# A two-block image kernel: softplus summed in PSUM, one product in ten moved from GpSimd to VectorE, large transfers cut into parts, background work spread

## The chip, the cores and the metric

The kernel runs on one core of a Trainium2 chip. The core has five engines with queues of their own: TensorE (PE, matrix products; the loading of its weights is listed apart as PEld), VectorE (DVE), ScalarE (ACT), GpSimd (POOL) and SyncE (SP, which here only issues transfers). Each engine works through its own list in order and waits on semaphores for the others. The metric is the device time of one execution in microseconds (us). It was 22,344.77 us in the median of three runs of the kernel before (22,316.2 to 22,348.97).

## The reference

The input is 16 images of 64 x 64 points with 96 channels, in float32. Two residual blocks follow one another. Each begins with a group normalisation of the image.

- Block one enlarges the image to twice its height and width by a band-limited interpolation, multiplies by a 384 x 96 matrix, applies a polynomial of degree two, multiplies by a 96 x 384 matrix, and filters and samples the result back to 64 x 64.
- Block two is a selective scan (a state-space layer). After a projection, a 3 x 3 convolution per channel and a SiLU, each image gives 192 channels of 4,096 points. They are read in four directions (rows, columns, and both backwards). In each direction there are 16 states per channel, and the recurrence along the 4,096 points is

```
delta = softplus(dts + bias)
h[t]  = exp(delta[t] * A) * h[t-1] + (delta[t] * u[t]) * B[t]
y[t]  = sum over the 16 states of h[t] * C[t]
```

The four results are added, normalised over the channels, multiplied by a gate, projected back to 96 channels and added to the image.

Only `softplus` and the product `h * C` are touched as arithmetic by the change. The kernel before and after computes softplus as max(s, 0) + ln(1 + e) - ((1 + e) - 1 - e) with e = exp(-|s|); the last term is the rounding error of 1 + e.

## The kernel before, in words

The time goes into `scan()` (lines 599 to 895). Everything else is either run before it (`front(0)`, the first image's preparation), after it (`finish(B - 1)`, the last image's end), or in the background of it.

**Units.** The work of the scan is cut into 3,072 units (`units`, line 699): 16 images, 8 steps in each (two pairs of directions times four pieces of 1,024 points), 6 blocks of channels and direction in a step, and 4 groups of states `j` in a block. A unit is a pair: two halves `e` of 128 partitions by 1,024 points. The loop at line 819 writes for each unit `n`, in this order:

- DVE: the recurrence of half 1 (`recur(n, 1, h)`, a TENSOR_TENSOR_SCAN at line 734 forwards or 736 backwards). Its decay `da` lies in PSUM, its drive `b` in SBUF, and it writes over `b`.
- PE: `read_out(n - 1)`, eight products that add the states of the unit before into `y` (line 758), then a background slot.
- ACT: `keep` (line 742), a copy of the last column of the state for the next piece, and `decay(n + 1, 1)` (line 719, exp of delta times A into one of two PSUM buffers).
- POOL: the product of half 1 with C (line 863, in place), and then `drive(n + 2)` (line 725, both halves of the drive of the unit after next, into one of three buffers `b`). This is "the odd product", and all that POOL does.
- DVE: the recurrence of half 0 (into the PSUM buffer of its decay), a second background slot, and the product of half 0 with C (line 873).
- ACT: `keep` and `decay(n + 1, 0)`; then a third slot.

A slot is thus met three times in a unit, at fixed places in the order of all engines.

**Background.** A slot advances generators by one `yield` (`Background`, lines 786 to 803). In each slot `project` of the next step may advance by one slice (60 slices spread over 58 slots, from the start of the step), and either `front` of the next image or, when that is done, `finish` of the image before may advance by one slice (404 slices over the 576 slots of an image). `front` and `finish` advance to the end when their result is due (`drain`).

**project** (lines 615 to 671) makes, for two halves of 512 points and three groups of channels, `delta` and `delta * u`. After a product on PE into `s` (line 643), each of these 768 projections runs through slots in order: ACT abs and exp (652, 653); ACT ln (655); DVE max and add (657); ACT 1 + e (659); DVE two operations (661, 662) that leave the softplus in PSUM; DVE times `u` (666); ACT copy (668); then both results are stored to memory through SP. The buffer `s` is single.

**front** and **finish.** `front` normalises (`norm`), runs block one in fine slices, then the convolution of block two (line 466, nine products for a tile, three in a slice). `finish` adds the four directions and does the output. Large transfers of up to 2 MB are single instructions on ACT's queue (`nc.scalar.dma_start`): the image `xt` (241), `s` (408), `x1` (431), `xs` (492), `ycol` (507, 508). All others are on SP's queue: the loads of `u` (627), the loads of `dtu` and `delta` (678) and of the rows B and C (687), and the stores of projections and results.

**Operands.** In the unit loop and in `project`, every DVE operation before has at most one input in SBUF; the other is in PSUM. Two small operations of the background have both in SBUF: `nb` (line 227, 96 x 1, twice an image) and `lin` (line 252, 96 x 96, once an image).

Of the kernel before, what the change touches and what calls it, by code (L numbers as in the profile page):

```python
# [70 lines left out]
POS = 3 * 8 * 6 * NQ  # L71
SLICES = 404
PSLICES = 60


@with_exitstack
def tile_two_blocks(
    ctx: ExitStack, tc: tile.TileContext,
    x, w1, w1t, b1, w2t, b2, coef, inpt, convw, convb, xpt, dtw, alog, dsk, onw, onb, opt,
    up, down, fold, ident, gmask, pmat, bumps, out,  # L80
# [29 lines left out]
    one_s = const.tile([128, 1], F32, name="one_s")  # L110
    nc.gpsimd.memset(one_s, 1.0)
    eps_g = const.tile([128, 1], F32, name="eps_g")
    nc.gpsimd.memset(eps_g, GEPS)
# [76 lines left out]
    def piece(shape, name):  # L190
        return b2p.tile(shape, F32, name=name, tag="piece")

    def norm(xt):

        s = small.tile([C, 8], F32, name="gs")
        for t in range(8):
            junk = piece([C, TB], "junk")
            nc.scalar.activation(junk, xt[:, TB * t:TB * t + TB], AF.Identity, accum_out=s[:, t:t + 1])
            if t % 2:
                yield  # L200
        yield
        m_ps = bank([C, 8], "m_ps")
        nc.tensor.matmul(m_ps, lhsT=gmask_s, rhs=s, start=True, stop=True)
        yield
        junk8 = small.tile([C, 8], F32, name="junk8")
        nmean = small.tile([C, 1], F32, name="nmean")
        nc.scalar.activation(junk8, m_ps, AF.Identity, scale=-1.0, accum_out=nmean)
        s2 = small.tile([C, 8], F32, name="gs2")
        for t in range(8):
            junk = piece([C, TB], "junk")  # L210
            nc.scalar.activation(
                junk, xt[:, TB * t:TB * t + TB], AF.Square, bias=nmean, accum_out=s2[:, t:t + 1]
            )
            if t % 2:
                yield
        yield
        v_ps = bank([C, 8], "v_ps")
        nc.tensor.matmul(v_ps, lhsT=gmask_s, rhs=s2, start=True, stop=True)
        yield
        var = small.tile([C, 1], F32, name="var")  # L220
        nc.scalar.activation(junk8, v_ps, AF.Identity, accum_out=var)
        rg = small.tile([C, 1], F32, name="rg")
        nc.scalar.activation(var, var, AF.Ln, bias=eps_g[0:C])
        nc.scalar.activation(rg, var, AF.Exp, scale=-0.5)
        nb = small.tile([C, 1], F32, name="nb")
        yield
        nc.vector.tensor_mul(nb, nmean, rg)
        yield
        return rg, nb

    def front(mi):

        x_c = x[mi].rearrange("h c w -> c h w")
        x_h = x[mi]
# [5 lines left out]
        xt = b16.tile([C, L], F32, name="xt", tag="b16")  # L240
        nc.scalar.dma_start(out=xt.rearrange("c (h w) -> c h w", w=HW), in_=x_c)
        for _ in range(4):
            yield
        rg, nb = yield from norm(xt)
# [160 lines left out]
        for _ in range(2):  # L405
            yield
        for i, on in enumerate((slice(0, JS), slice(JS, HW))):
            nc.scalar.dma_start(out=s[i], in_=s_d[:, on, :])
        for _ in range(8):
            yield  # L410
        x1 = xt
        x1v = x1.rearrange("c (h w) -> c h w", w=HW)
        done = None
        for j0 in range(0, HW + 8, 8):
# [15 lines left out]
            yield  # L430
        nc.scalar.dma_start(out=made["x1"], in_=x1)
        rg, nb = yield from norm(x1)
# [12 lines left out]
        for i, n, tiles, both in ((0, 128, 8, 0), (1, 64, 4, 4)):  # L445
            col = b16.tile([128, tiles * TB], F32, name="col", tag="b16")
            parts = [(n * k, t0) for k, t0 in enumerate((0, both)[:128 // n])]
            turned = None

            def turn(t, row, z):  # L450
                nc.scalar.copy(
                    col.rearrange("c (w h) -> c w h", w=HW)[:, :, 8 * t:8 * t + 8],
                    row.rearrange("c (h w) -> c w h", w=HW),
                )
                for p, t0 in parts:
                    cols = slice(TB * (t + t0), TB * (t + t0) + TB)
                    nc.sync.dma_start(out=made["xs"][2 * i, 0:n, cols], in_=row[p:p + n])
                    nc.sync.dma_start(out=made["z"][128 * i:128 * i + n, cols], in_=z[p:p + n])

            for t in range(tiles):  # L460
                c_ps = bank([128, 8, HW], "c_ps")
                for tap in range(9):
                    dy, dx = divmod(tap, 3)
                    for p, t0 in parts:
                        h0 = 8 * (t + t0) + dy
# [7 lines left out]
                    if tap % 3 == 2 and tap < 8:  # L473
                        yield
                z_ps = bank([128, 8, HW], "z_ps")
                for p, t0 in parts:
                    h0 = 8 * (t + t0) + 1
# [3 lines left out]
                    )  # L481
                yield
                row, z = piece([128, TB], "row"), piece([128, TB], "z")
# [3 lines left out]
                turned = t, row, z  # L487
                yield
            turn(*turned)
            yield  # L490
            if i == 0:
                nc.scalar.dma_start(out=made["xs"][1], in_=col)
            else:
                for p, t0 in parts:
                    to = made["xs"][2, 64:128, :].rearrange("c (w h) -> c w h", h=HW)
                    for w0 in range(0, HW, 16):
# [3 lines left out]
                        )  # L500
                        yield

    def finish(mi):

        y_d, xs_d, z_d, x1_d = (image[mi][k] for k in ("y", "xs", "z", "x1"))
        ycol = [b18.tile([128, L], F32, name="ycol0", tag="b18"), b16.tile([64, L], F32, name="ycol1", tag="b16")]
        nc.scalar.dma_start(out=ycol[0], in_=y_d[1, 0:128, :])
        nc.scalar.dma_start(out=ycol[1], in_=y_d[1, 128:DI, :])

# [9 lines left out]
        ahead = fetch_y(0)  # L519
        for _ in range(6):  # L520
            yield
        tail = None
        for t in range(8):
# [7 lines left out]
            for ob, n in ((0, 128), (1, 64)):  # L531
# [8 lines left out]
                if ob == 1:  # L540
                    sq.append(piece([128, TB], "sq"))
                    nc.scalar.activation(sq[0], yc[0], AF.Square)
                yield
                for i in range(2):
# [10 lines left out]
                yc.append(y_ps.rearrange("c h w -> c (h w)"))  # L555
                yield

# [3 lines left out]
            nc.tensor.matmul(v_ps, lhsT=mean_s, rhs=sq[0], start=True, stop=False)  # L561
            yield
            yz.append(piece([64, TB], "yz"))
            nc.vector.tensor_mul(yz[1], yc[1], z1)
            nc.tensor.matmul(v_ps, lhsT=mean_s[0:64], rhs=sq[1], start=False, stop=True)
            if t < 7:
                ahead = fetch_y(t + 1)
            yield
            r = sq[0][0:C]
# [3 lines left out]
            for i, n in ((0, 128), (1, 64)):  # L573
                nc.tensor.matmul(o_ps, lhsT=ow_s[0:n, i, :], rhs=yz[i], start=(i == 0), stop=(i == 1))
            yield
            e_ps = bank([C, TB], "oe_ps")
            for i, (w, of) in enumerate(((ob_s[:, 0, :], z0), (ob_s[0:64, 1, :], z1), (ident_s[0:C, 0:C], xt))):
                nc.tensor.matmul(e_ps, lhsT=w, rhs=of, start=(i == 0), stop=False)  # L578
            nc.vector.tensor_mul(r, o_ps, r)
            yield  # L580

# [9 lines left out]
        for _ in tail:  # L591
            yield

# [5 lines left out]
    def scan():  # L599


        with ExitStack() as es:
# [12 lines left out]
            def project(mi, pair, lc, out):  # L615
# [7 lines left out]
                for t in range(0, T, TB):  # L623
# [15 lines left out]
                    for i, v in enumerate((0, 2, 1)):  # L639
# [9 lines left out]
                        yield  # L649
                        e = pj.tile([128, TB], F32, name="e")  # L650
                        d = pj.tile([128, TB], F32, name="d")
                        nc.scalar.activation(e, s, AF.Abs)
                        nc.scalar.activation(e, e, AF.Exp, scale=-1.0)
                        yield
                        nc.scalar.activation(d, e, AF.Ln, bias=one_s)  # L655
                        yield
                        nc.vector.scalar_tensor_tensor(d, s, 0.0, d, ALU.max, ALU.add)  # L657
                        yield
                        nc.scalar.activation(s, e, AF.Identity, bias=one_s)
                        yield  # L660
                        nc.vector.scalar_tensor_tensor(s, s, -1.0, e, ALU.add, ALU.subtract)
                        nc.vector.tensor_sub(s, d, s)
                        yield
# [122 lines left out]
            class Background:  # L786


                def __init__(self, gen, slices, positions):
                    self.gen, self.slices, self.positions, self.at, self.n = gen, slices, positions, 0, 0  # L790

                def slot(self):
                    self.at += 1
                    if self.gen is not None and self.n * self.positions < self.at * self.slices:
                        self.n += 1
                        if next(self.gen, 0) == 0:
                            self.gen = None

                def drain(self):
                    while self.gen is not None:  # L800
                        self.n += 1
                        if next(self.gen, 0) == 0:
                            self.gen = None

# [14 lines left out]
            for n, (st, bi, j) in enumerate(units):  # L819
# [41 lines left out]
                if n < last:  # L861
                    decay(n + 1, 1)
                nc.gpsimd.tensor_mul(h, h, bc[1, r, j])  # L863
                if n + 2 <= last:
                    drive(n + 2)

                h = das[n, 0]
                recur(n, 0, h)
                if n and units[n - 1][2] == NQ - 1:
                    storing = store(n - 1)  # L870
# [75 lines left out]
def _layout(i):  # L946
# [4 lines left out]
    for k in range(ND):  # L951
# [12 lines left out]
    laid = {  # L964
        "x": x,
        "w1": w1.reshape(HB, 128, C).swapaxes(0, 1),
        "w1t": w1.T,
# [35 lines left out]
```

## Time and profile before

One execution was profiled. Its own time was 22,310.87 us and its span 22,309.1 us; the median of the runs is 34 us above it.

| | us | share of the span |
|---|---|---|
| span | 22,309.1 | |
| POOL busy, 6,152 instructions | 20,896.4 | 94% |
| DVE busy | 19,837.0 | 89% |
| PE busy (matmul) | 15,814.4 | 71% |
| ACT busy | 13,129.1 | 59% |
| before the first unit's recurrence | 538 | 2% |
| units (538 to 22,144 us) | 21,606 | 97% |
| after the last | 166 | 1% |

The page lists the busy time of each engine, then groups of instructions: source line, engine, operation, output <- inputs, shapes, the count, the busy time and the mean duration in ns, and the idle time of the engine just before them with what ended it. Lists of waits give the engine and line that waited, what it waited for, the total in us, the number of times and the longest. A table of windows gives the busy time of every engine in a stretch, and behind it the clock granted to PE as a share of full speed (PEclk) and the share of the DMA engines that was busy.

### The profile page before, as it was taken

The numbers are of one execution on the slowest core, as the hardware profiler recorded it, in microseconds if no ns is written. First come the engines' busy times: TensorE is split into PE (matmuls) and PEld (weight loads), VectorE is DVE, ScalarE is ACT, GpSimd is POOL, SyncE is SP. The second block draws the span as 40 slices with busy tenths as digits, with TensorE's granted clock in tenths as the row PEclk, the third lists the DMA queues.
The fourth block names the chain that finished last, engine by engine and source line by source line (L and its number), as shares of the span: only waits on it lengthen the run. The fifth ranks groups of instructions, "written<-read, shape, count | busy, mean of one in ns | idle before, by whom it ended". The sixth has DMA issues, their size and how long they took to land.

```text
span 22309.1 us, 261027 instructions
## 1 busy us (share of the span) xinstructions
PE 15814.4 (71%) x92844; PEld 6455.6 (29%) x92844; DVE 19837.0 (89%) x12829; ACT 13129.1 (59%) x20854; POOL 20896.4 (94%) x6152
## 2 busy tenths in 40 slices
PE   6675777767778677776777777677786777767745
PEld 4322323223232322323223232332323223232211
DVE  0999999899998999989899898999989999898996
ACT  3665655656556565565656556565565655656543
POOL 0999999999999999999999999999999999999997
PEclk7676777877778677686777878677786776867856
DMA  2555565655656556565655656556565665656654
GB/s 77 185 194 184 191 210 182 209 191 193 206 189 210 184 198 204 190 210 186 203 194 191 210 184 209 192 189 209 189 212 184 201 201 190 210 186 203 211 177 133
DMA packets 1915769, 4276.30 MB, mean 192 GB/s; under 512 B 543454, under 2 KB 642686, under 8 KB 1906206
## 3 DMA queue, kind: packets, MB, share of 16 engines
q1 hardware_dynamic: 1804702, 4086.06, 54.6%
q10 hardware_dynamic: 109760, 173.55, 3.0%
q8 instruction: 731, 11.98, 0.2%
q14 instruction: 576, 4.72, 0.1%
HBM read 3380.58 MB, written 878.18 MB: 191 GB/s over the span
## 4 chain that ended last, share of the span: by engine, by line
POOL 31%; issue 20%; DVE 20%; PE 15%; DMA 8%; ACT 5%; SPq 1%; POOLq 0%; ACTq 0%; DVEq 0%
POOL b L863 15%; POOL b L725 15%; DVE da L736 4%; DVE b L734 4%; DVE da L734 4%; DVE b L736 3%; DVE b L873 3%; PE y L758 2%; PE c_ps L466 2%; DMA u<-xs_d 2%; PE pp L633 2%; ACT da L719 2%; PE yc L535 1%; DMA ct<-rows 1%; PE oe_ps L578 1%
## 5 line engine op out<-in xcount | busy, mean ns | idle before, releaser
L725 POOL TENSOR_TENSOR b<-dtu,bt 128x2048 f32<-128x2048 f32 x3072 | 14000.3, 4557 | 578.3 <-DMA dtu<-dtu_d 531.9
L758 PE MATMUL y<-b,fold_s 128*32 128x256 f32 x49152 | 4865.1, 506 | 4962.9 <-DVE b L873 3489.3
L719 ACT ACTIVATE da<-delta,a_s 128x1024 f32<-128x1024 f32 x6144 | 6855.9, 1116 | 2487.3 <-DVE b L873 1350.0
L863 POOL TENSOR_TENSOR b<-b,ct 128x1024 f32<-128x1024 f32 x3072 | 7323.1, 2384 | 668.3 <-ACT new L742 591.3
L758 PEld LDWEIGHTS y<-b,fold_s 128*32 128x32 f32 x49152 | 1324.5, 127 | 8709.7 <-DVE b L873 4353.2
L873 DVE TENSOR_TENSOR b<-da,ct 128x1024 f32<-128x1024 f32 x3072 | 3750.4, 1221 | 75.1
L736 DVE TENSOR_TENSOR_SCAN b<-da,new,b 128x1024 f32<-128x1024 f32 x1152 | 2697.2, 2341 | 376.5 <-ACT new L742 223.5
L734 DVE TENSOR_TENSOR_SCAN b<-da,new,b 128x1024 f32<-128x1024 f32 x1152 | 2700.9, 2344 | 288.4 <-POOL b L725 283.4
L736 DVE TENSOR_TENSOR_SCAN da<-da,new,b 128x1024 f32<-128x1024 f32 x1152 | 2692.7, 2337 | 108.4 <-ACT da L719 108.4
L734 DVE TENSOR_TENSOR_SCAN da<-da,new,b 128x1024 f32<-128x1024 f32 x1152 | 2693.5, 2338 | 85.3 <-ACT da L719 85.3
L742 ACT COPY new<-da 128x1 f32<-128x1 f32 x2304 | 362.6, 157 | 3347.7 <-DVE b L873 3344.4
L466 PE MATMUL c_ps<-xgp,wtap_s 96*128 96x512 f32 (+1 forms) x4608 | 1676.9, 625 | 119.1 <-ACT row L484 114.5
L643 PE MATMUL s<-pr,dtw_s 128*128 128x512 f32 x1536 | 1202.3, 875 | 244.6 <-ACT delta L668 212.5
L358 PE MATMUL h_ps<-xu,w1t_s 96*128 96x500 f32 x1920 | 1316.4, 798 | 74.3 <-ACT hsq L341 32.8
L633 PE MATMUL pp<-u,xpt_s 128*128 128x512 f32 x1536 | 1061.8, 844 | 372.9 <-DMA u<-xs_d 359.8
L370 PE MATMUL o_ps<-w2c_s,hsq 128*100 128x96 f32 x9600 | 1222.0, 296 | 25.8 <-ACT new L742 15.1
L370 PEld LDWEIGHTS o_ps<-w2c_s,hsq 128*100 128x100 f32 x9600 | 1154.6, 208 | 284.9 <-issue 186.6
L742 ACT COPY new<-b 128x1 f32<-128x1 f32 x2304 | 429.9, 187 | 1058.2 <-DVE b L734 587.7
L657 DVE SCALAR_TENSOR_TENSOR d<-s,d 128x512 f32<-128x512 f32 x768 | 521.8, 679 | 555.6 <-ACT d L655 553.1
L736 DVE TENSOR_TENSOR_SCAN da<-da,b 128x1024 f32<-128x1024 f32 x384 | 876.5, 2282 | 133.5 <-ACT da L719 133.5
L734 DVE TENSOR_TENSOR_SCAN b<-da,b 128x1024 f32<-128x1024 f32 x384 | 876.2, 2282 | 99.3 <-POOL b L725 65.7
L736 DVE TENSOR_TENSOR_SCAN b<-da,b 128x1024 f32<-128x1024 f32 x384 | 876.5, 2283 | 69.8 <-POOL b L725 65.5
(120 smaller groups left out, 18395.2 us busy)
## 6 DMA issues: line engine op xcount, KB each, us to landing
dtu<-dtu_d SPq DMA_DIRECT2D x1536, 512.0 KB
delta<-delta_d SPq DMA_DIRECT2D x1536, 512.0 KB
bt<-rows SPq DMA_DIRECT2D x1024, 512.0 KB
ct<-rows SPq DMA_DIRECT2D x1024, 512.0 KB
u<-xs_d SPq DMA_DIRECT2D x896, 256.0 KB
dtu_d<-dtu SPq DMA_DIRECT2D x768, 256.0 KB
delta_d<-delta SPq DMA_DIRECT2D x768, 256.0 KB
xr<-in_x SPq DMA_DIRECT2D x768, 128.0 KB
```

What stands on the lines that cost most here:

```text
L358: nc.tensor.matmul(h_ps[j], lhsT=w1t_s[:, 128 * j:128 * (j + 1)], rhs=xu.rearrange("c p q -> c (p q)"), start=True, stop=True,)
L370: nc.tensor.matmul(o_ps[:, p, :], lhsT=hsq[j][:, UPS * p:UPS * (p + 1)], rhs=w2c_s[:, j, :], start=(j == 0), stop=(j == HB - 1),)
L466: nc.tensor.matmul(c_ps[p:p + n], lhsT=wtap_s[:, tap, 128 * i:128 * i + n], rhs=xgp[:, h0:h0 + 8, dx:dx + HW], start=(tap == 0), stop=(tap ...
L633: nc.tensor.matmul(pp, lhsT=xpt_s[:, pair, v, :], rhs=u[v], start=(v == 0), stop=(v == 2))
L643: nc.tensor.matmul(s, lhsT=dtw_s[:, pair, v, :], rhs=pr, start=True, stop=True)
L719: nc.scalar.activation(da, ops["delta", n // NQ][:, e, :], AF.Exp, scale=a_s[:, k, g, units[n][2]:units[n][2] + 1])
L725: nc.gpsimd.tensor_mul(b, ops["dtu", n // NQ], bt.unsqueeze(1).to_broadcast([128, 2, T]))
L734: nc.vector.tensor_tensor_scan(out, da, b, before, ALU.mult, ALU.add)
L736: nc.vector.tensor_tensor_scan(out[:, ::-1], da[:, ::-1], b[:, ::-1], before, ALU.mult, ALU.add)
L758: nc.tensor.matmul(y[32 * q:32 * q + 32, e, :], lhsT=fold_s, rhs=b[:, e, QT * q:QT * q + QT], start=(pair == 0 and j == 0 and e == 0), sto ...
L863: nc.gpsimd.tensor_mul(h, h, bc[1, r, j])
L873: nc.vector.tensor_mul(bs[n][:, 0, :], h, bc[1, r, j])
```

## The change

Four things change together.

- **Softplus.** The three DVE operations of a projection (657, 661, 662) go. ACT makes max(s, 0) (`m`, a Relu) and w = (1 + e) - 1 in two steps, and PE adds the four terms, e - w + ln(1 + e) + max(s, 0), in PSUM: four products of 128 x 128 with the identity or minus the identity (`less_i`), each of 512 points. DVE's product with `u` reads that sum from PSUM, one slot later. A projection has seven slots in place of eight; a step's `project` has 52 yields in place of 58, and 54 slices over 58 slots are set in place of 60.
- **One odd product in five.** In every fifth unit (614 of 3,072) the product of half 1 with C is made by DVE, after its recurrence of half 0 and ahead of the slot and of its product of half 0. Both its inputs, `bs` and `bc`, are in SBUF. POOL goes on from `drive(n + 1)` to `drive(n + 2)`.
- **Large transfers.** The ones on ACT's queue become two to six pieces each on SP's queue, with a yield after each piece. The image is loaded from an input `xc` that the host has laid out by channel.
- **Spreading.** The slices of the convolution and of `finish` yield a weight of 2. 540 in place of 404 weights are spread over an image's 576 slots. By the yields in the code, `front` takes 324 slices before and 389 weights after (461 and 415 slots), and `finish` 73 slices before and 142 weights after (about 104 and 152 slots). After the change both together fill 567 of the 576 slots.

```diff
-SLICES = 404
-PSLICES = 60
+SLICES = 540
+HEAVY = 2
+PSLICES = 54
+SHARE = 5
...
+    less_s = const.tile([128, 1], F32, name="less_s")
+    nc.gpsimd.memset(less_s, -1.0)
+    less_i = const.tile([128, 128], F32, name="less_i")
+    nc.vector.tensor_scalar(less_i, ident_s, -1.0, None, ALU.mult)
...
+    def parts(out, in_, n=4):
+
+        step = L // n
+        for i in range(n):
+            nc.sync.dma_start(out=out[:, step * i:step * i + step], in_=in_[:, step * i:step * i + step])
+            yield
...
-        nc.scalar.dma_start(out=xt.rearrange("c (h w) -> c h w", w=HW), in_=x_c)
-        for _ in range(4):
-            yield
+        yield from parts(xt, xc[mi])
+        yield
...
-        for i, on in enumerate((slice(0, JS), slice(JS, HW))):
-            nc.scalar.dma_start(out=s[i], in_=s_d[:, on, :])
-        for _ in range(8):
+        for i, n, first in [(0, JS // 4, k * JS // 4) for k in range(4)] + [(1, 10, 0), (1, 10, 10)]:
+            nc.sync.dma_start(out=s[i][:, first:first + n, :], in_=s_d[:, JS * i + first:JS * i + first + n, :])
             yield
+        yield
...
-        nc.scalar.dma_start(out=made["x1"], in_=x1)
+        yield from parts(made["x1"], x1)
...
                     if tap % 3 == 2 and tap < 8:
-                        yield
+                        yield HEAVY
...
-                nc.scalar.dma_start(out=made["xs"][1], in_=col)
+                yield from parts(made["xs"][1], col)
...
-        nc.scalar.dma_start(out=ycol[0], in_=y_d[1, 0:128, :])
-        nc.scalar.dma_start(out=ycol[1], in_=y_d[1, 128:DI, :])
+        yield from parts(ycol[0], y_d[1, 0:128, :])
+        yield from parts(ycol[1], y_d[1, 128:DI, :], 2)
...
-                        e = pj.tile([128, TB], F32, name="e")
-                        d = pj.tile([128, TB], F32, name="d")
+                        e, d, m, w = (pj.tile([128, TB], F32, name=k) for k in ("e", "d", "m", "w"))
                         nc.scalar.activation(e, s, AF.Abs)
                         nc.scalar.activation(e, e, AF.Exp, scale=-1.0)
                         yield
+                        nc.scalar.activation(m, s, AF.Relu)
+                        nc.scalar.activation(w, e, AF.Identity, bias=one_s)
+                        yield
                         nc.scalar.activation(d, e, AF.Ln, bias=one_s)
+                        nc.scalar.activation(w, w, AF.Identity, bias=less_s)
                         yield
-                        nc.vector.scalar_tensor_tensor(d, s, 0.0, d, ALU.max, ALU.add)
-                        yield
-                        nc.scalar.activation(s, e, AF.Identity, bias=one_s)
-                        yield
-                        nc.vector.scalar_tensor_tensor(s, s, -1.0, e, ALU.add, ALU.subtract)
-                        nc.vector.tensor_sub(s, d, s)
+                        s = gps.tile([128, TB], F32, name="s", tag="g")
+                        for k, (sign, of) in enumerate(((less_i, w), (ident_s, e), (ident_s, d), (ident_s, m))):
+                            nc.tensor.matmul(s, lhsT=sign, rhs=of, start=(k == 0), stop=(k == 3))
                         yield
...
                 def slot(self):
                     self.at += 1
                     if self.gen is not None and self.n * self.positions < self.at * self.slices:
-                        self.n += 1
-                        if next(self.gen, 0) == 0:
-                            self.gen = None
+                        self.step()
+
+                def step(self):
+                    weight = next(self.gen, 0)
+                    if weight == 0:
+                        self.gen = None
+                    else:
+                        self.n += weight or 1
...
-                nc.gpsimd.tensor_mul(h, h, bc[1, r, j])
+                odd_here = n % SHARE == SHARE - 1
+                if not odd_here:
+                    nc.gpsimd.tensor_mul(h, h, bc[1, r, j])
                 if n + 2 <= last:
                     drive(n + 2)
 
                 h = das[n, 0]
                 recur(n, 0, h)
+                if odd_here:
+                    nc.vector.tensor_mul(bs[n][:, 1, :], bs[n][:, 1, :], bc[1, r, j])
...
+        "xc": x.transpose(0, 2, 1, 3).reshape(-1, C, L),
```

## The prediction

> **What bounds the kernel now.** I read the busy times first, then windows over stages, then groups, waits, and single stretches of the timeline. Windows: the units as a whole (538 to 22,144 us), the convolution of one image, a hole behind it, its `finish`, and a stretch of block one.
>
> ```profile
> 538.00:22144.00 21606.00, 15297.59 (x90302) 6185.94 (x90302) 19795.96 (x12744) 12896.94 (x20486) 20890.83 (x6143) 0.74 0.59 195
> 8200.00:8300.00 100.00, 89.47 (x423) 33.40 (x421) 88.20 (x54) 79.38 (x113) 95.46 (x29) 0.95 0.66 227
> 8370.00:8384.00 14.00, 4.73 (x14) 1.94 (x18) 3.54 (x3) 0.30 (x1) 3.48 (x1) 0.56 0.88 207
> 8400.00:8560.00 160.00, 148.35 (x585) 45.20 (x582) 151.94 (x106) 86.49 (x127) 154.51 (x46) 0.91 0.69 224
> 8800.00:9000.00 200.00, 144.12 (x1005) 70.01 (x1002) 185.14 (x116) 120.23 (x205) 200.00 (x60) 0.72 0.52 177
> ```
>
> The columns are length, then busy PE, PEld, DVE, ACT, POOL, then PE's clock, DMA share and GB/s. In block one POOL is busy 200 of 200 us: it is the bound, at 20,891 / 3,072 = 6.80 us a unit. It idles 715 us (21,606 - 20,891) among the units, all in the heavier stages. At 8,370 it stood still: the chain of waits there names the load of `ycol` (12.8 us), behind it `u`, then PE, ACT's `keep`, POOL. DVE is second, 19,796 us busy.
>
> ```profile
> L725 POOL TENSOR_TENSOR b<-dtu,bt 128x2048 f32<-128x2048 f32 x3072 | 14000.3, 4557 | 578.3 <-DMA dtu<-dtu_d 531.9 <-PE y L758 21.2 <-issue 9.6
> L863 POOL TENSOR_TENSOR b<-b,ct 128x1024 f32<-128x1024 f32 x3072 | 7323.1, 2384 | 668.3 <-ACT new L742 591.3 <-DVE b L736 65.7 <-DMA u<-xs_d 4.8
> L873 DVE TENSOR_TENSOR b<-da,ct 128x1024 f32<-128x1024 f32 x3072 | 3750.4, 1221 | 75.1
> L662 DVE TENSOR_TENSOR s<-d,s 128x512 f32<-128x512 f32 x768 | 534.4, 696 | 26.3
> L661 DVE SCALAR_TENSOR_TENSOR s<-s,e 128x512 f32<-128x512 f32 x768 | 521.9, 680 | 65.7 <-ACT s L659 65.7
> L657 DVE SCALAR_TENSOR_TENSOR d<-s,d 128x512 f32<-128x512 f32 x768 | 521.8, 679 | 555.6 <-ACT d L655 553.1 <-ACT new L742 1.6
> ```
>
> The reader is to see what one POOL operation and one softplus operation cost. Next, what DVE waits for:
>
> ```profile
> DVE d L657 <- ACT d L655: 553.1, 222, 127.6
> DVE da L736 <- ACT da L719: 242.0, 152, 4.5
> DVE b L736 <- ACT new L742: 225.9, 75, 13.9
> DVE da L734 <- ACT da L719: 146.5, 80, 5.1
> DVE yz L554 <- ACT sq L542: 94.7, 23, 26.5
> DVE b L736 <- ACT da L719: 74.0, 37, 4.2
> DVE yz L564 <- ACT sq L560: 72.2, 24, 6.5
> ```
>
> Of these 463 us wait for a decay and 167 for `finish`: they stay. The longest wait of the first row, 127.6, lies before the units. And the two DVE operations with both inputs in SBUF, with one stretch of the timeline:
>
> ```profile
> L227 DVE TENSOR_TENSOR nb<-nmean,rg x32: 155/1601/9002, 44.5 to 20306.0; 96x1 f32<-96x1 f32 x32
> L252 DVE TENSOR_TENSOR lin<-lin,ident_s x16: 245/2191/2196, 45.3 to 19543.7; 96x96 f32<-96x96 f32 x16
> 4046.56 4.50 POOL L725 TENSOR_TENSOR b<-dtu,bt 128x2048 f32<-128x2048 f32 x1
> 4048.84 9.00 DVE L227 TENSOR_TENSOR nb<-nmean,rg 96x1 f32<-96x1 f32 x1
> 4051.03 2.33 POOL L863 TENSOR_TENSOR b<-b,ct 128x1024 f32<-128x1024 f32 x1
> 4053.34 4.48 POOL L725 TENSOR_TENSOR b<-dtu,bt 128x2048 f32<-128x2048 f32 x1
> ```
>
> `nb` multiplies one element per partition. It took 0.155 us before POOL had work, and 1.6 us in the median beside it; here 9.00, until POOL's third operation ended. In all 45 cases beside POOL it or `lin` ended 0.02 to 0.11 us after a POOL operation's end. So two SBUF inputs wait for POOL. The moved product has two SBUF inputs.
>
> **The change part by part**, within the units:
>
> *POOL* loses 614 products of 6.80 - 4.50 = 2.30 us each (4.50 is the drive's duration in the timeline): 1,412 us, leaving 19,479. What DVE's product costs POOL, if it is held up in turn, no row shows (after `lin` POOL shows no delay, but `lin` is short): 0 to 1.22 us each, L873's duration, 0 to 750 us; I take 750, since the wait is seen in the other direction. POOL's floor is 20,229.
>
> *DVE* loses 521.8 + 521.9 + 534.4 = 1,578 us and gains 614 x 1.221 = 750: 18,968 busy. Kept waits 630: 19,598. Gone are the waits of 657 and 661 (425 + 66) and most of the 226 of the `ycol` hole.
>
> *The new wait of DVE for PE's sum.* Paired row by row, the 756 projections after the first step give means, from the start of `s`: exp ends at 4.08 us, ln ends 2.20 later, and the operation of line 661, five slots behind `s`, starts at 11.44. After the change ln stands a slot later and 1 + e - 1 behind it (0.68): the last operand is there at 4.08 + 2.20 + 2.20 + 0.68 = 9.16. Then PE streams four products, eight rows. L643's rows, of the same shape and each with weights of its own, start 0.52 us apart at full clock and 1.00 at half, so 4.2 to 8.0; at a clock of 0.9, as where PE is busiest, 4.6. The sum is ready at 13.8. DVE's product with `u` now holds the fifth slot, 11.44: it waits 2.3 us, and queued behind it on DVE stand the product of half 0 or the next recurrence; ACT's decay and PE's `read_out` wait for those. 768 x 2.3 = 1,766. Five slots are 1.67 units, so one projection in three has a moved product within them, which covers its wait: 1,178. Bounds: 0 if PE and ACT run ahead, 768 x 5.7 = 4,378 at half clock throughout.
>
> *The new wait of the moved product for POOL.* 48 `nb` and `lin`, of which 45 beside POOL, took 91.7 + 33.1 us: 2.7 a piece, with 9.0 at worst and 0 as the other end (POOL idle). POOL will idle somewhat more, so 2.0: 614 x 2.0 = 1,228 (0 to 5,526). Behind it stand the product of half 0, the next recurrence, and POOL's next odd product, which needs that recurrence.
>
> The Trainium skill, SBUF — State Buffer, section "Who interferes with whom", says that a VectorE instruction with two SBUF inputs and a GpSimd instruction that reads SBUF exclude each other for a whole instruction, in order of issue. It speaks against this change. By it the wait would be the rest of one drive, half of 4.50 as an estimate, 1,380 us for 614. The 9.00 of `nb`, through three POOL operations, is not what it leads one to expect.
>
> *PE* gets 6,144 rows: 3,195 us at full clock, 6,132 at half, 3,533 at 0.9. 15,298 + 3,533 = 18,831, 86% of the units' time: hidden as throughput; without that cover it is the third rival. *ACT* gains a Relu like line 652 (586 ns) and another Identity like 659 (676): 768 x 1.26 = 969, to 13,866, 63%.
>
> The Trainium skill, TensorE: Matmul & The Clock Gate, Part 1, says that sustained work releases the clock to full. The windows agree (0.95 at 89% busy, 0.72 at 72%). By it alone the eight rows take 4.2 us, the wait 1.9, and the sum falls by about 200 us.
>
> *Transfers.* SP issues 24 pieces an image in place of ACT's 7: 272 more, at some 0.4 us (`ycol`'s issues took 0.34 and 0.47) 109 us. SP is no bound: it waited 4,954 us for `dtu` alone. A piece of a quarter of `ycol` takes some 2 us; behind it in SP's queue are `u`, `dtu`, `delta` and the rows of B and C, fetched several units ahead. What goes is POOL's idling at three places of an image, 12.0, 4.7 and 2.0 us in the mean of 14 images: 15 x 18.7 = 280. It enters as the dropped 226 on DVE. *Spreading* lowers the convolution's and `finish`'s rate by a third and raises block one's from 0.70 to 0.94 of the slots; I cost it at nothing, since PE's total is unchanged; if block one's cover goes, it shows in the DVE waits above.
>
> **Sum.** DVE: 19,598 + 1,178 + 1,228 = 22,004, above POOL's 20,229. With 538 before and 166 after: 22,708, against 22,309 of the profiled execution; 34 us more for the median: 22,740, 1.8% above 22,344.77. DVE becomes the bound; the break-even is 21,606 - 19,598 = 2,008 us for both new waits together, 2,406 taken.
>
> **The rivals.** First, the wait for POOL costs little (DVE's request falls at the end of a drive, or POOL idles): 19,598 + 1,178 + 704 = 21,480, and 21,510 with the 34. For it: 15 of 30 `nb` waited only 1.6. Against: POOL has the next drive ready without waiting, so a missed end costs 4.5. It decides below 1.35 us a product (830 / 614). Second, the sum of PE is early: 19,598 + 1,228 = 20,826, over POOL's 20,229 plus its remaining idling (715 - 280) = 20,664; with 704 and 34, 21,560. For it: ACT's row of slots is short in block one. Against: the 9.16 + 4.2 above. Third, PE's queue is the bound, its clock staying near half: 15,298 + 6,132 = 21,430 at the 0.957 that PE reaches at most (units 176 to 183 of an image, mean of 14): 22,393 + 738 = 23,130. For it: 0.74 as mean clock. Against: 0.91 to 0.95 where PE is busy.
>
> **How the numbers follow.** The forecast 0.50 (22,350 to 23,350 for itself, each wait half as large or as large again), the first 0.21, the second 0.17, the third 0.12. The first two are faster; from the forecast's lower edge come 0.01 faster and 0.03 the same. Within 0.2% is about what a measurement of this kernel can tell from no change. Faster 0.38, same 0.04, slower 0.58. The range 21,200 to 23,550 leaves out a tenth on each side: both new waits small, or the third with longer waits.
>
> **What would show it.** DVE's product with `u` waiting for PE, in total near 1,200 us; the moved product lasting about 3.2 us in place of 1.22, ending after POOL's drives; POOL idle over 10% of the units and waiting for ACT's `keep` and DVE; PE's clock over 0.85; no hole at `ycol`. Wrong it would be if the moved product lasts under 2 us, or PE's sum stands ready when DVE comes.

## The result and the profile after

The changed kernel took 24,150.2 us in the median of four runs (24,134 to 24,181) against 22,346.9 us (now four runs of the kernel before): 1.0811 times the time before, 95% interval 1.0792 to 1.0830. The forecast had said slower, by 1.8%; it is 8.1%, outside the range of 21,200 to 23,550.

Windows over the units of the changed kernel's profile (545 to 23,969 us; length, busy PE, PEld, DVE, ACT, POOL, then PE's clock, DMA share, GB/s):

```profile
545.00:23969.00 23424.00, 17269.63 (x96398) 7249.82 (x96398) 20378.35 (x11071) 13651.36 (x22011) 19734.06 (x5530) 0.81 0.54 180
```

POOL idles 3,690 of 23,424 us (the length less its busy time), five times as long as before; it is no longer the bound. DVE stands higher, at 20,378 us. The groups that answer to those shown of before, from the changed kernel's page:

```profile
L736 POOL TENSOR_TENSOR b<-dtu,bt 128x2048 f32<-128x2048 f32 x3072 | 14106.4, 4599 | 853.8 <-DMA dtu<-dtu_d 540.2
L880 POOL TENSOR_TENSOR b<-b,ct 128x1024 f32<-128x1024 f32 x2458 | 5786.9, 2354 | 3375.9 <-ACT new L753 2580.2
L892 DVE TENSOR_TENSOR b<-da,ct 128x1024 f32<-128x1024 f32 x3072 | 3749.2, 1220 | 70.9
L677 DVE TENSOR_TENSOR dtu<-s,u 128x512 f32<-128x512 f32 x768 | 529.9, 690 | 2455.8 <-PE s L673 2432.7
L887 DVE TENSOR_TENSOR b<-b,ct 128x1024 f32<-128x1024 f32 x614 | 2163.5, 3524 | 73.1 <-ACT new L753 71.8
L673 PE MATMUL s<-w,less_i 128*128 128x512 f32 x1536 | 1289.6, 934 | 1084.7 <-ACT w L669 1003.8
```

Two lines tell the story. L677, the product of softplus with `u`, makes DVE idle 2,456 us, almost all of it for PE's sum. L887, the moved product, lasts 3,524 ns, while the same shape with one operand in PSUM (L892) lasts 1,220. The list of DVE's waits:

```profile
DVE dtu L677 <- PE s L673: 2432.7, 677, 138.3
DVE da L745 <- ACT da L730: 231.6, 191, 2.4
DVE da L747 <- ACT da L730: 215.6, 138, 4.7
DVE b L747 <- ACT da L730: 92.9, 68, 4.1
DVE b L887 <- ACT new L753: 71.8, 65, 3.6
DVE b L745 <- ACT da L730: 56.3, 53, 22.2
DVE b L747 <- POOL b L736: 27.0, 32, 1.1
DVE b L745 <- POOL b L736: 21.7, 33, 0.9
```

The columns are total us, times, longest. Six waits of the first row, 204 us in all, lie before the first unit, so 2,229 us lie within. DVE waits for POOL only 49 us, against 493 before:

```profile
DVE b L734 <- POOL b L725: 349.1, 474, 1.1
DVE b L736 <- POOL b L725: 144.3, 187, 1.1
```

Within the units DVE has 20,378 us of work, 2,229 of waits for the sum, 574 for decays (22 more lie before the units), 72 for `keep` ahead of the moved product and 49 for POOL: 23,302 of the units' 23,424 us; the rest is small gaps. Work and idle time fill the units on any engine, so this sum alone does not make DVE the bound, as was forecast; e2 and e5 below do, where DVE's waits are cut and the time falls.

How the moved product waits, in two stretches of the timeline (some rows of DVE left out). The first:

```profile
10095.04 2.37 POOL L880 TENSOR_TENSOR b<-b,ct 128x1024 f32<-128x1024 f32 x1
10097.35 10.01 POOL L736 TENSOR_TENSOR b<-dtu,bt 128x2048 f32<-128x2048 f32 x2
10099.58 3.40 DVE L887 TENSOR_TENSOR b<-b,ct 128x1024 f32<-128x1024 f32 x1
10102.90 1.21 DVE L892 TENSOR_TENSOR b<-da,ct 128x1024 f32<-128x1024 f32 x1
```

DVE comes to L887 2.2 us into POOL's first drive, waits to its end at 10,101.9, and then runs. The second drive is held up: the two together last 10.01 us. In the second stretch they last 8.99:

```profile
10018.39 8.99 POOL L736 TENSOR_TENSOR b<-dtu,bt 128x2048 f32<-128x2048 f32 x2
10023.21 5.25 DVE L887 TENSOR_TENSOR b<-b,ct 128x1024 f32<-128x1024 f32 x1
10028.98 1.21 DVE L892 TENSOR_TENSOR b<-da,ct 128x1024 f32<-128x1024 f32 x1
10030.11 2.33 DVE L745 TENSOR_TENSOR_SCAN b<-da,new,b 128x1024 f32<-128x1024 f32 x1
10032.53 2.35 POOL L880 TENSOR_TENSOR b<-b,ct 128x1024 f32<-128x1024 f32 x1 [5.15 <-DVE b L745]
```

Here DVE came 0.3 us after the handover from the first drive to the second, waited 4.2 us for the second, and POOL then had nothing to do for 5.15 us, until DVE had made the recurrence that POOL's next product needs. Counted over the trace, of 614 moved products 225 ran between two drives, 317 after POOL's last ready drive with POOL then idle, 46 were passed by a whole POOL operation, and 26 did not wait.

### The profile page after: what moved, and what is told of

It reads as the page before. It is cut to its first block, busy times and chain, and to the rows that moved or that the text cites. A ratio compares the mean times of both kernels' runs of the same rounds, so it can differ in the third digit from the quotient of the medians.

```text
span 24132.7 us, 274164 instructions
## 1 busy us (share of the span) xinstructions
PE 17808.6 (74%) x98988; PEld 7528.0 (31%) x98988; DVE 20407.6 (85%) x11140; ACT 13888.9 (58%) x22390; POOL 19739.0 (82%) x5539
## 5 line engine op out<-in xcount | busy, mean ns | idle before, releaser
L880 POOL TENSOR_TENSOR b<-b,ct 128x1024 f32<-128x1024 f32 x2458 | 5786.9, 2354 | 3375.9 <-ACT new L753 2580.2
L769 PE MATMUL y<-b,fold_s 128*32 128x256 f32 x49152 | 4193.0, 464 | 4130.1 <-DVE b L892 3776.3
L892 DVE TENSOR_TENSOR b<-da,ct 128x1024 f32<-128x1024 f32 x3072 | 3749.2, 1220 | 70.9
L677 DVE TENSOR_TENSOR dtu<-s,u 128x512 f32<-128x512 f32 x768 | 529.9, 690 | 2455.8 <-PE s L673 2432.7
L887 DVE TENSOR_TENSOR b<-b,ct 128x1024 f32<-128x1024 f32 x614 | 2163.5, 3524 | 73.1 <-ACT new L753 71.8
L673 PE MATMUL s<-w,less_i 128*128 128x512 f32 x1536 | 1289.6, 934 | 1084.7 <-ACT w L669 1003.8
L369 PE MATMUL h_ps<-xu,w1t_s 96*128 96x500 f32 x1920 | 1100.5, 679 | 155.8 <-ACT hsq L352 123.5
L673 PE MATMUL s<-e,ident_s 128*128 128x512 f32 x1536 | 1163.1, 852 | 0.0
L381 PE MATMUL o_ps<-w2c_s,hsq 128*100 128x96 f32 x9600 | 1055.2, 271 | 77.8 <-ACT hsq L352 63.2
L654 PE MATMUL s<-pr,dtw_s 128*128 128x512 f32 x1536 | 892.4, 664 | 185.2 <-ACT delta L679 133.1
L673 PE MATMUL s<-d,ident_s 128*128 128x512 f32 x1536 | 970.9, 720 | 0.0
```

The lines of the kernel that those rows point to most:

```text
L369: nc.tensor.matmul(h_ps[j], lhsT=w1t_s[:, 128 * j:128 * (j + 1)], rhs=xu.rearrange("c p q -> c (p q)"), start=True, stop=True,)
L381: nc.tensor.matmul(o_ps[:, p, :], lhsT=hsq[j][:, UPS * p:UPS * (p + 1)], rhs=w2c_s[:, j, :], start=(j == 0), stop=(j == HB - 1),)
L673: nc.tensor.matmul(s, lhsT=sign, rhs=of, start=(k == 0), stop=(k == 3))
L769: nc.tensor.matmul(y[32 * q:32 * q + 32, e, :], lhsT=fold_s, rhs=b[:, e, QT * q:QT * q + QT], start=(pair == 0 and j == 0 and e == 0), sto ...
L887: nc.vector.tensor_mul(bs[n][:, 1, :], bs[n][:, 1, :], bc[1, r, j])
L892: nc.vector.tensor_mul(bs[n][:, 0, :], h, bc[1, r, j])
```

## The experiments

Each time stands beside the kernel before on the same chip; the last column is the ratio's 95% interval.

| run | softplus | moved product | other | us | to before, 95% |
|---|---|---|---|---|---|
| after | PE | 1 in 5, SBUF | pieces, spread | 24,150 | 1.0792 to 1.0830 |
| e1 | PE | none | pieces, spread | 23,035 | 1.0302 to 1.0333 |
| e2 | PE, read a slot later | 1 in 5, SBUF | pieces, spread | 23,244 | 1.0397 to 1.0431 |
| e3 | DVE | 1 in 5, SBUF | pieces, spread | 23,290 | 1.0419 to 1.0450 |
| e4 | DVE | none | pieces, spread | 21,939 | 0.9811 to 0.9841 |
| e5 | PE | 1 in 5, PSUM | pieces, spread | 22,956 | 1.0266 to 1.0300 |
| e6 | PE, covered | none | pieces, spread | 22,150 | 0.9909 to 0.9939 |
| e7 | PE, covered | 1 in 5, PSUM | pieces, spread | 21,565 | 0.9648 to 0.9676 |
| e8 | DVE | 1 in 10, PSUM | pieces, spread | 21,917 | 0.9804 to 0.9833 |
| e9 | DVE | none | pieces | 22,170 | 0.9901 to 0.9934 |
| e10 | PE, two terms, later | 1 in 5, PSUM | pieces, spread | 21,127 | 0.9440 to 0.9468 |
| e11 | PE, covered | 1 in 7, PSUM | pieces, spread | 21,673 | 0.9685 to 0.9714 |
| e12 | PE, covered | 1 in 4, PSUM | pieces, spread | 21,490 | 0.9603 to 0.9635 |

Theory A is the prediction's: DVE is the bound through two new waits, for PE's sum and for POOL. Theory B: PE's added rows are the bound. Theory C: the spreading or SyncE's queue. "Covered" in the table means that two of the four terms are added a slot earlier and the sum is read a slot later (e6).

### One part at a time: e1, e3, e4, e9

e1, all odd products on POOL:

```diff
-SHARE = 5
+SHARE = 1000000000
```

> The changed kernel with every odd product back on GpSimd; softplus on TensorE, transfers and spreading stay. Theory A (VectorE's two new waits are the cost): the 614 moved products go, 2,163 us of VectorE time with their waits for GpSimd, and GpSimd gets 614 x 2.30 = 1,412 us back, so that its own work of 20,891 us and VectorE's of about 21,200 us (18,200 busy, 2,290 waiting for the sum, 700 other waits) lie side by side: 21,900 to 22,500 us. Theory B (TensorE's added 6,144 rows are the bound): 23,900 to 24,200 us, since TensorE's work is unchanged. Theory C (spreading and the pieces on SyncE's queue do the harm): 23,500 us or more.

e3, softplus on DVE as before, with `PSLICES = 60`; the diff undoes the change's:

```diff
...
-                        nc.scalar.activation(m, s, AF.Relu)
-                        nc.scalar.activation(w, e, AF.Identity, bias=one_s)
-                        yield
                         nc.scalar.activation(d, e, AF.Ln, bias=one_s)
-                        nc.scalar.activation(w, w, AF.Identity, bias=less_s)
                         yield
-                        s = gps.tile([128, TB], F32, name="s", tag="g")
-                        for k, (sign, of) in enumerate(((less_i, w), (ident_s, e), (ident_s, d), (ident_s, m))):
-                            nc.tensor.matmul(s, lhsT=sign, rhs=of, start=(k == 0), stop=(k == 3))
+                        nc.vector.scalar_tensor_tensor(d, s, 0.0, d, ALU.max, ALU.add)
+                        yield
+                        nc.scalar.activation(s, e, AF.Identity, bias=one_s)
+                        yield
+                        nc.vector.scalar_tensor_tensor(s, s, -1.0, e, ALU.add, ALU.subtract)
+                        nc.vector.tensor_sub(s, d, s)
                         yield
```

> The changed kernel with softplus on VectorE as before (60 slices); one odd product in five on VectorE, transfers and spreading stay. Theory A: VectorE has 19,796 + 750 us of work, about 614 x 2.3 = 1,410 us of waiting for GpSimd in the moved products and 1,000 us of other waits, 22,960 us, and 700 us around the units: 23,300 to 23,900 us. Theory B: TensorE is relieved of the 6,144 rows, below 22,400 us. Theory C: 23,900 us or more.

e4, both edits together.

> The changed kernel with softplus on VectorE and every odd product on GpSimd: the transfers in pieces and the spreading of the background are all that is left of the change. Theory A: the hole at the loads of ycol goes, 15 x 18.7 = 280 us: 21,950 to 22,150 us. Theory B: the same. Theory C: 23,000 us or more. No effect of either: 22,350 us.

e9, e4 without the weights:

```diff
-SLICES = 540
-HEAVY = 2
+SLICES = 404
+HEAVY = 1
```

> e4 without the spreading: softplus on VectorE, every odd product on GpSimd, every slice of weight 1 and 404 slices over an image's 576 slots as before; the large transfers in pieces on SyncE's queue are all that is left of the change. If the pieces make e4's gain: 22,000 to 22,100 us (280 us of holes). If the spreading makes it: 22,250 to 22,350 us, with GpSimd idling in the convolution and in finish as before.

Pieces and spreading together gain 1.7%, and theory C is out. The pieces alone gain 0.8%: POOL's idling at the loads of `ycol` falls from 12.0 to 2.1 us an image. With the spreading POOL's gaps of over 0.2 us, summed by image and averaged over 14, come to 24.5 us, against 39.8 in e9 and 48.2 before; 15 x 15.3 = 230 us, which covers the second half of the gain (0.9% by the ratios). e9's 22,170 lies between what the two readings expected: both parts count.

On e4, softplus on PE alone costs 1,096 us, the moved product alone 1,351, both 2,211. e3 came 10 us below the range expected. e1 missed its range by 535 us, and its waits tell why (DVE's, the largest and those for POOL):

```profile
DVE dtu L677 <- PE s L673: 2823.6, 757, 137.5
DVE b L747 <- POOL b L736: 243.6, 323, 2.0
DVE b L745 <- POOL b L736: 227.1, 247, 1.1
```

Without any moved product DVE waits for PE's sum in 757 of 768 projections, 2,618 us within the units. POOL was busy 20,921 of the units' 22,309 us. Neither engine is full: DVE loses its lead while a step's projections run, and waits for POOL again (471 us) when they are done: 407 of the 471 us lie in the last two and the first three of a step's 24 units, and the waits for the sum in units 3 to 17. The sum of one engine's work is then too low a bound.

### The wait for the sum: e2, e6

e2 lets DVE come a slot later; every engine has the same work:

```diff
-PSLICES = 54
+PSLICES = 60
...
                             nc.tensor.matmul(s, lhsT=sign, rhs=of, start=(k == 0), stop=(k == 3))
                         yield
+                        yield
                         dtu = pj.tile([128, TB], F32, name="dtu")
```

> The changed kernel with one more slot between TensorE's sum and VectorE's product with u (60 slices in place of 54 over 58 slots, so that a step's projections still fit). The same work on every engine. Theory A: the product with u stands some 2.4 us later, so the mean wait for the sum falls from 2.9 to about 1 us, in total from 2,220 to 700 us, and the time to 22,500 to 23,000 us. Theory B: no change, 24,000 to 24,300 us. Theory C: no change.

e6 is e1 with that slot, and with two of the four terms added a slot earlier:

```diff
                         nc.scalar.activation(d, e, AF.Ln, bias=one_s)
                         nc.scalar.activation(w, w, AF.Identity, bias=less_s)
-                        yield
                         s = gps.tile([128, TB], F32, name="s", tag="g")
-                        for k, (sign, of) in enumerate(((less_i, w), (ident_s, e), (ident_s, d), (ident_s, m))):
-                            nc.tensor.matmul(s, lhsT=sign, rhs=of, start=(k == 0), stop=(k == 3))
+                        for k, of in enumerate((e, m)):
+                            nc.tensor.matmul(s, lhsT=ident_s, rhs=of, start=(k == 0), stop=False)
+                        yield
+                        for k, (sign, of) in enumerate(((ident_s, d), (less_i, w))):
+                            nc.tensor.matmul(s, lhsT=sign, rhs=of, start=False, stop=(k == 1))
+                        yield
                         yield
```

> Every odd product on GpSimd, as in e1, but the sum of softplus is taken out of VectorE's way: TensorE adds e and max(s, 0) a slot earlier and only the other two terms in the old slot, and VectorE's product with u stands one slot later. TensorE and ScalarE do the same work as in e1. Theory A (it is the wait for the sum that costs): VectorE's wait for it falls from 2,690 to under 500 us, GpSimd is the bound at 20,900 us and some 250 us of idling: 21,750 to 22,050 us, at or a little below e4's 21,939. Theory B (TensorE's added rows or ScalarE's added operations hold the others up): 22,500 us or more.

e2 gains 906 us with the same work on PE, so theory B is not what holds the changed kernel. Its wait for the sum fell to 859 us within the units, a little less than expected, and the time lies 244 us over the range: part of the gain came back as waits for decays, 961 us in place of 596 (DVE's list in e2):

```profile
DVE dtu L678 <- PE s L673: 1065.6, 512, 138.3
DVE da L748 <- ACT da L731: 403.3, 204, 5.9
DVE da L746 <- ACT da L731: 311.9, 288, 2.0
DVE b L746 <- ACT da L731: 170.8, 121, 22.4
DVE b L748 <- ACT da L731: 74.8, 72, 2.7
```

e6 takes 885 us off e1, and the wait falls from 2,618 to 342 us within the units. But at 22,150 us it is 100 us over its range and 211 above e4: DVE waits 1,082 us for decays there, and POOL 378 us for ACT's `keep`, against 208 in e4. With POOL the bound, softplus on PE brings nothing by itself, even when the wait for it is covered.

### The wait for POOL: e5

In every fifth unit the recurrence of half 1 writes to PSUM, and the moved product reads it there:

```diff
-                h = bs[n][:, 1, :]
+                odd_here = n % SHARE == SHARE - 1
+                h = das[n, 1] if odd_here else bs[n][:, 1, :]
                 recur(n, 1, h)
+                if odd_here:
+                    nc.vector.tensor_mul(bs[n][:, 1, :], h, bc[1, r, j])
...
-                odd_here = n % SHARE == SHARE - 1
                 if not odd_here:
...
-                if odd_here:
-                    nc.vector.tensor_mul(bs[n][:, 1, :], bs[n][:, 1, :], bc[1, r, j])
```

> The changed kernel, but in every fifth unit the recurrence of half 1 writes over its decay in PSUM, as that of half 0 does, and VectorE's moved product reads it there, right behind that recurrence: one input in PSUM, one in SBUF; the decay of half 1 of the next unit is issued behind it. Theory A (the moved product waits for GpSimd because both its inputs are in SBUF): it takes 1.22 us in place of 3.52, 614 x 2.30 = 1,410 us less on VectorE: 22,500 to 23,000 us. Theory D (it is long for another reason, such as the dependence on ScalarE's keep or on its place): it stays above 2 us and the time near 24,100 us. Theory E (the third buffer of decays is missed: ScalarE's decay of the next unit now starts after the moved product): the decay's waits on VectorE grow by more than 600 us and the time stays above 23,300 us.

The moved product's line in the changed kernel and then in e5 (duration minimum, median, maximum in ns):

```profile
L887 DVE TENSOR_TENSOR b<-b,ct x614: 1202/3444/7897, 583.1 to 23954.4; 128x1024 f32<-128x1024 f32 x154
```

```profile
L874 DVE TENSOR_TENSOR b<-da,ct x614: 1223/1225/1227, 582.5 to 22776.7; 128x1024 f32<-128x1024 f32 x154
```

It takes 1.225 us with 4 ns between the fastest and the slowest, though 596 of the 614 ran beside a POOL operation, 571 of them for nearly their whole length. POOL's drives are not held up either: none takes over 4.61 us. The time falls by 1,194 us, of 1,410 expected; the list's wait for the sum grew by 81 us meanwhile (2,514 in place of 2,433). Theory D is out, and E too: the waits for decays stay at 577 us. The edit also moves the product ahead of the recurrence of half 0; that its duration depends on the operand is shown, that the place has no share in the time is not.

### Both covered, and how far it goes: e7, e8, e10, e11, e12

e7 joins e5 and e6's softplus, with `SHARE = 5`. e8 is e4 with e5's edit and `SHARE = 10`. e11 and e12 are e7 with `SHARE = 7` and `SHARE = 4`.

> e5's PSUM operand and e6's softplus together, one odd product in five on VectorE. Theory A: both new waits are gone; VectorE has 18,220 + 750 us of work and about 1,000 us of waits, GpSimd 19,480 us; they share the bound: 20,900 to 21,500 us, below e4. Theory B (TensorE's added rows then bound it): 22,000 us or more.

> e4 (softplus on VectorE, transfers and spreading) with e5's PSUM operand for one odd product in ten. VectorE gets 307 x 1.22 = 375 us, GpSimd loses 307 x 2.30 = 706. Theory A: GpSimd 20,190, VectorE 20,170 and about 900 us of waits: 21,550 to 21,900 us. If any moved product costs more than it saves: 22,000 us or more.

> e7 with one odd product in seven on VectorE (438 in place of 614). GpSimd's work rises by 176 x 2.30 = 405 us to 19,920, VectorE's falls by 176 x 1.22 = 215 us. If VectorE with its waits is e7's bound: 21,350 to 21,550 us. If GpSimd is: 21,600 to 21,900 us.

> e7 with one odd product in four on VectorE (768 in place of 614). GpSimd's work falls by 154 x 2.30 = 354 us, VectorE's rises by 154 x 1.22 = 188 us. By e11, where one in seven lost 110 us against e7, GpSimd is the closer bound: 21,400 to 21,550 us. If VectorE has taken its place: 21,600 us or more.

e7 is 3.4% below the kernel before, 65 us above its range. e11's and e12's numbers are those expected with GpSimd as the closer bound; e8 is 17 us over its range. One product in four (e12) gives 21,490 us, 3.8% below; one in seven 21,673. The gain of the moved product is there once both waits are cut: e6 to e7, 585 us. Where softplus stays on DVE (e8), one in ten gives nothing that can be told from e4 (0.9819 and 0.9826 of the time before). What holds e7 up shows in its waits (DVE's, then POOL's; 300 us of the first row lie within the units):

```profile
DVE dtu L680 <- PE s L675: 487.4, 227, 135.4
DVE da L750 <- ACT da L733: 363.1, 214, 5.9
DVE da L748 <- ACT da L733: 292.5, 271, 5.3
POOL b L885 <- ACT new L756: 845.0, 486, 10.5
```

By these lists the two others now wait most for ACT: DVE 892 us for decays, POOL 845 for `keep`. ACT in turn waits 3,385 us for DVE's product of half 0 (2,387 before `keep`, 998 before decays), so the lists alone do not say which engine is late. e10 takes work from ACT and PE (the diff is against the changed kernel; e5's edit, the added `yield` and `PSLICES = 60` are not shown):

```diff
-                        e, d, m, w = (pj.tile([128, TB], F32, name=k) for k in ("e", "d", "m", "w"))
+                        e, d, m = (pj.tile([128, TB], F32, name=k) for k in ("e", "d", "m"))
...
                         nc.scalar.activation(m, s, AF.Relu)
-                        nc.scalar.activation(w, e, AF.Identity, bias=one_s)
                         yield
                         nc.scalar.activation(d, e, AF.Ln, bias=one_s)
-                        nc.scalar.activation(w, w, AF.Identity, bias=less_s)
                         yield
...
-                        for k, (sign, of) in enumerate(((less_i, w), (ident_s, e), (ident_s, d), (ident_s, m))):
-                            nc.tensor.matmul(s, lhsT=sign, rhs=of, start=(k == 0), stop=(k == 3))
+                        for k, (sign, of) in enumerate(((ident_s, d), (ident_s, m))):
+                            nc.tensor.matmul(s, lhsT=sign, rhs=of, start=(k == 0), stop=(k == 1))
```

> e5's PSUM operand with VectorE's product one slot later, as in e2, and the sum reduced to ln(1 + e) + max(s, 0): the term that corrects the rounding of 1 + e is left out, with two of TensorE's four products (3,072 rows) and ScalarE's two operations for it (768 x 1.29 = 990 us). To be set beside e7, where the sum is whole. If TensorE's and ScalarE's added work still costs e7 time, by decays that come late: VectorE's waits for decays fall from 890 us to under 600 and the time to 21,100 to 21,400 us. If they are hidden there: 21,500 to 21,650 us.

It reaches 21,127 us, 5.5% below before, as expected. Waits for decays fall to 675 us (892 in e7; under 600 was expected), POOL's for ACT's `keep` to 540. So the added work of PE and ACT still costs e7 about 440 us. Which of the two it is was not separated: e10 takes from both, and it also adds the terms in one slot in place of two. It is no replacement of the whole sum, as it leaves a term out.

## Why the prediction was wrong

**Right: the mechanism and the bound.** DVE took the bound from POOL through the two waits named, the moved product's and the sum's; all the marks given for it but two are in the trace (PE's clock among the units is 0.81, not over 0.85, and the sum's wait is nearly twice the size named).

**Wrong: the term "768 x 2.3 = 1,766 ... covers its wait: 1,178".** It measured 2,229 us, 1,051 of the 1,420 us by which the units outlasted the sum of 22,004 (23,424). Both its factors were too kind.

- *The wait of one projection*, uncovered, is what e1 shows: 3.46 us in the mean of 756, from three small errors of one sign. Paired as in the prediction, e1 has the last operand at 9.52 us (9.16 taken), the sum at 14.74 (13.8) and DVE's place at 11.31 (11.44). From the last operand the sum took 5.2 us and not 4.6: 0.3 until its first product and 4.9 for the four. The clock granted during the sums was 0.78 and not 0.9; half of them began at half clock, and the 275 that had full clock throughout took 3.7 us.
- *The cover*: of the 756 projections after the change, 359 had a moved product between the start of `s` and DVE's product, nearly one in two and not one in three. But they still waited, 2.39 us in the mean; the other 397 waited 3.44, as in e1. Beside a moved product DVE's place lies 3.4 us later (14.79 against 11.38), but the last operand lies 1.8 us later too (11.43 against 9.65), and the sum 2.0 (16.76 against 14.78). So a moved product covers 1.0 of the 3.4 us and not the whole; in total the wait fell by 15% (2,618 us in e1 to 2,229) and not by a third. ACT's operations of softplus stand in its queue behind decays and `keep` that wait for the same held-up DVE: ACT waits 6,294 us for DVE's product of half 0 after the change, against 4,402 in e1.

```profile
ACT new L753 <- DVE b L892: 4558.4, 1726, 10.3
ACT da L730 <- DVE b L892: 1735.2, 607, 9.0
```

A wait that delays the engine delays the chain feeding it, too.

**Nearly right: the wait of the moved product.** 2.30 us each, 1,414 in total, for 2.0 and 1,228: off by 186 us. The rows of `nb` and `lin` foretold both its size and its mechanism.

**The other waits of DVE** came to some 817 us, 187 more than the 630 that were kept. Of the 167 kept for `finish`, 118 lay behind the last unit in the profile before, where the 166 us after the units hold them already. The 425 us of line 657, called gone, were 392 within the units: six of its waits, 161 us, lie before the first, and not only the longest. That figure does not enter the sum.

**POOL held up in turn** was taken at 1.22 us each: it measured 1.0 (drives of 5.50 in place of 4.50 us), but in only 225 of 614 cases. In the others POOL idled outright, which the sum over DVE contains.

**The range** does not follow from its words, each wait "half as large or as large again": 23,350 is 610 us above the sum of 22,740, about half of one wait, while both waits as large again give 25,150. Bounds of 4,378 and 5,526 us had been worked out; the upper end of the first alone gives 25,940.

**The transfers** held in kind: POOL's hole at `ycol` is down from 12.0 to 2.1 us an image (e9), but the pieces gave 166 us where 280 were expected. **The spreading**, costed at nothing, gains 0.9% by the ratios of e9 and e4, some 205 us. The first two rivals are excluded by the time itself, but e5 and e2 show the price of their conditions, 1,194 and 906 us. The third, PE as the bound at 23,130 us, is refuted by e7, which has the same products on PE and takes 21,565 us; e2 shows that PE's work does not set the time of the changed kernel.

## What to carry to other kernels

Before work is moved to another engine, look up where the operands lie: the same product took 3.52 us with both inputs in SBUF beside a busy GpSimd and 1.22 with one in PSUM; in the first form moving it cost 1,351 us (e4 to e3), in the second, with the sum covered, it gained 585 (e6 to e7). Work taken off an engine is no gain if that engine then waits in order for the result: compare the ready time of the last operand plus the producer's duration with the consumer's place in its queue, and give the consumer one more slot, or feed the producer earlier. Where a wait is put against another wait as its cover, ask whether the second delays the first one's inputs too.

## What the runs showed of the hardware

- VectorE's product with both inputs in SBUF and GpSimd's products exclude each other, in both directions. 582 of the 614 ended 1.08 us (1.08 to 1.10 from the first to the 99th of a hundred) behind the end of a GpSimd operation, and a GpSimd drive that was next in line lasted 5.50 in place of 4.50 us. With one input in PSUM (e5) neither was held up. This agrees with the Trainium skill, SBUF — State Buffer, section "Who interferes with whom".
- The turn does not always go to the one that came first: 46 of the 614 were passed by one more GpSimd operation, with up to 7.9 us in the product; 35 of them had stood ready for 0.3 us or more when that operation began. The order of issue, which the prediction quotes, does not foretell them.
- PE's granted clock rose from 0.74 to 0.81 in the mean of the units with the added rows, and to 0.85 in e7. The Trainium skill, TensorE: Matmul & The Clock Gate, Part 1, lets sustained work release the clock; the direction agrees, but with PE busy 74% of the time full clock was granted for part of it only: the four products of a sum took 5.0 us in the mean (4.9 in e1), against 3.7 for those at full clock throughout.
